# Layer 3 of a four-layer graph network: the 0/1 mask of edges and slots is copied to PSUM and read there by VectorE's products

## The chip, the core and the metric

The kernel runs on one core of one Trainium2 chip. A core has five engines that work in parallel, each through its own queue of instructions: TensorE (PE, matrix products), VectorE (DVE), ScalarE (ACT), GpSimd (POOL, which here issues all gathers and scatters by index) and SyncE (SP, which issues the plain transfers). The metric is the device time of one execution in microseconds (us); lower is better. Operands lie in HBM, in SBUF (the working memory of 128 partitions) or in PSUM (the memory that TensorE writes its results to[...]).

## The reference, cut to what matters

A graph of 12,500 nodes and 212,500 edges goes through four layers, each followed by a layer norm of the sum with its input. Layers 0 to 2 are a weighted sum over edges, an edge network with batch norms, and two graph convolutions. Layer 3, which the change touches, makes six steps. In each, every edge has a 32x32 matrix of its own, made from its attributes by a small network, and multiplies its source node's state; the messages are summed per destination and update the node by a GRU:

```python
eh = relu(e_feat @ en1_w.T + en1_b)                    # (edges, 128)
w_e = (eh @ en2_w.T + en2_b).reshape(-1, D, D)         # D = 32
for _ in range(STEPS):                                 # 6
    msg = einsum('ei,eio->eo', out[src], w_e)
    agg = segment_sum(msg, dst, num_segments=n_nodes) + conv_bias
    h = gru_cell(relu(agg), h, ...)
    out = h
```

## The kernel before, in words

The edges are first sorted by destination, and padded to 212,992: 128 partitions times J = 1664 columns. A column holds 128 neighbouring edges of the sorted order, one per partition, and these have at most 13 destinations (W); otherwise another branch runs, which this input doesn't take. Within a column, each edge has a slot of 0 to 12 for its destination. A chunk is CB = 32 columns, and there are NCH = 52 chunks.

`slot_sum` (line 838) walks over the chunks, for layer 2's convolutions and for each step of layer 3. For each chunk VectorE makes the `mask` (line 848): for 128 edges, 32 columns and 13 slots it is 1 where the edge has that slot. It has three buffers in SBUF. Then a function `fill` puts the sums per slot into `acc` in PSUM, and `then` (line 857) carries them across columns: `on` (L858), a copy out of `acc` by ScalarE (L869), a running sum (`s`, L871), a reordering (L881), eight small matmuls (`back`, L888), and a store.

For layer 3 `fill` is the one in `conditioned` (line 1047). It never makes the edges' matrices. With `eh` (128 values per edge, stored once in HBM) and the gathered states `g`, each half of a chunk (16 columns) goes so:

- POOL gathers the rows of the table `t3` into `g`, one indirect DMA for each column (helper `gather`, L258), so 16 per half and 32 per chunk. A row has the state (32 values) and the state times the bias matrix (32 more). `g` has three buffers of half a chunk.
- SyncE loads `eh` for the half (L1064), also with three buffers.
- For each pair of columns, VectorE multiplies states and mask into `prod` (L1068): for each of 2 columns, 32 features times 13 slots, 832 values per partition. TensorE multiplies `eh` by `prod` into `m` in PSUM (L1076, one matmul for each column; the profile has each fp32 matmul as two records), and ScalarE moves `m` to `outer` in SBUF (L1083). `prod` and `m` have two buffers each.
- The second matmuls of a half (`second`: L1094, 32 of them with `outer` and the weights `en2_i`, and L1104, 16 with `g` and `mask`) are put off until the following half's pairs have been issued, and after the second half of a chunk they are followed by `then`.

Between the loops of two steps lie 98 gathers of the slot ends into `agg` (L258 again), the GRU, and the writing of a new `t3`.

The order within each engine's queue is not written out by hand: the framework's scheduler makes it from the program's order, the dependencies and the free buffers, and puts in the waits. So three masks are made at the beginning of a step, and from then on, in the middle of a chunk, the mask of the chunk after next, beside the `on` and `s` of earlier chunks. [...]

The `mask` is read at two places: by the products (L1068) and by the matmuls of L1104.

Of the kernel before, what the change touches and what calls it, by code (L numbers as in the profile page):

```python
# [32 lines left out]
F32 = mybir.dt.float32  # L33
# [3 lines left out]
AF = mybir.ActivationFunctionType  # L37
# [4 lines left out]
P = 128  # L42
# [4 lines left out]
CB = 32  # L47
# [7 lines left out]
F = 32  # L55
# [3 lines left out]
W = 13  # L59
CW = CB * W  # L60
HB = CB // 2
# [10 lines left out]
def tile_gnn(ctx: ExitStack, tc: tile.TileContext, a: dict, out: bass.AP):  # L72
    nc = tc.nc
# [5 lines left out]
    def sb(pool, shape, dt, name, **kw):  # L79
        return pool.tile(shape, dt, name=name, tag=name, **kw)  # L80
# [488 lines left out]
    with ExitStack() as by_source:  # L569
# [98 lines left out]
        with ExitStack() as l1:  # L668
            n1 = l1.enter_context(tc.tile_pool(name="n1b", bufs=1))
            work = l1.enter_context(tc.tile_pool(name="l1", bufs=3))  # L670
# [167 lines left out]
    def slot_sum(name, rows, table, fill, agg):  # L838


        with tc.tile_pool(name=f"sl_{name}", bufs=2) as work, tc.tile_pool(
            name=f"slp_{name}", bufs=2, space=PSUM
        ) as psum:
            prev = [None]

            def one(c):
                mask = sb(work, [P, CB, W], F32, "mask", bufs=3)
                nc.vector.tensor_tensor(  # L848
                    mask,
                    slot[:, c * CB : (c + 1) * CB].unsqueeze(2).to_broadcast([P, CB, W]),  # L850
                    iota_w.unsqueeze(1).to_broadcast([P, CB, W]),
                    op=ALU.is_equal,
                )
                acc = sb(psum, [rows, CB, W], F32, "acc")

                def then():
                    on = sb(work, [rows, W, CB + 1], F32, "on")
                    nc.vector.tensor_tensor(  # L858
                        on,
                        going[0:rows, c, :].unsqueeze(1).to_broadcast([rows, W, CB + 1]),  # L860
                        iota_w[0:rows, :].unsqueeze(2).to_broadcast([rows, W, CB + 1]),
                        op=ALU.is_equal,
                    )
                    part_ = sb(work, [rows, W, CB + 1], F32, "part")
                    if prev[0] is None:
                        nc.vector.memset(part_[:, :, 0:1], 0.0)
                    else:
                        nc.vector.tensor_copy(part_[:, :, 0], prev[0][:, :, CB])
                    nc.scalar.activation(part_[:, :, 1:], acc.rearrange("p t w -> p w t"), AF.Copy)  # L869
                    s = sb(work, [rows, W, CB + 1], F32, "s")  # L870
                    nc.vector.tensor_tensor_scan(  # L871
                        s.rearrange("p w t -> p (w t)"),
                        on.rearrange("p w t -> p (w t)"),
                        part_.rearrange("p w t -> p (w t)"),
                        initial=0.0,
                        op0=ALU.mult,
                        op1=ALU.add,
                    )
                    prev[0] = s
                    by8 = sb(work, [rows, CB // 8, W, 8], F32, "by8")  # L880
                    nc.scalar.activation(  # L881
                        by8.rearrange("p b w t -> p w b t"),
                        s[:, :, 1:].rearrange("p w (b t) -> p w b t", t=8),
                        AF.Copy,
                    )
                    back = sb(psum, [R8, CB // 8, F], F32, "back", bufs=1)
                    for b in range(CB // 8):
                        nc.tensor.matmul(  # L888
                            back[:, b, :],
                            by8[:, b].rearrange("p w t -> p (w t)"),  # L890
                            stack[0:rows, :],
                            start=True,
                            stop=True,
                        )
                    o = sb(work, [R8, CB // 8, F], F32, "o")
                    nc.scalar.activation(o, back, AF.Copy)
                    n = CB // 8
                    nc.sync.dma_start(
                        table[0:SLOTS, :].rearrange("(r b) f -> r b f", r=R8)[:, c * n : (c + 1) * n, :], o
                    )  # L900

                fill(work, psum, c, mask, acc, then)

            for c in range(NCH):
                one(c)
            fill(None, None, None, None, None, None)
        for c in range(NH):
            gather(agg[:, c, :], table, slot_end[:, c : c + 1])

# [122 lines left out]
                new_table()  # L1032

    def convolved(name, table, nr, agg):
        def fill(work, psum, c, mask, acc, then):
            if work is None:
                return
            g = sb(work, [P, CB, F], F32, "g", bufs=3)
            for j in range(CB):
                gather(g[:, j, :], tables[table], idx_d[:, c * CB + j : c * CB + j + 1])  # L1040
            for j in range(CB):
                nc.tensor.matmul(acc[:, j, :], g[:, j, :], mask[:, j, :], start=True, stop=True)  # L1042
            then()

        slot_sum(f"l2{name}", F, sums[nr], fill, agg)

    def conditioned(agg):
        waiting = []

        def fill(work, psum, c, mask, acc, then):  # L1050
            def flush():
                while waiting:
                    waiting.pop(0)()

            if work is None:
                flush()
                return
            for b in range(2):
                t0 = c * CB + b * HB
                g = sb(work, [P, HB, 2 * F], F32, "g", bufs=3)  # L1060
                for j in range(HB):
                    gather(g[:, j, :], tables["t3"], idx_d[:, t0 + j : t0 + j + 1])
                eh = sb(work, [P, HB, EH], F32, "eh", bufs=3)
                nc.sync.dma_start(eh, edge_h[:, t0 : t0 + HB, :])  # L1064
                outer = sb(work, [EH, F, HB, W], F32, "outer")
                for j in range(0, HB, 2):
                    prod = sb(work, [P, 2, F, W], F32, "prod")
                    nc.vector.tensor_tensor(  # L1068
                        prod,
                        g[:, j : j + 2, 0:F].unsqueeze(3).to_broadcast([P, 2, F, W]),  # L1070
                        mask[:, b * HB + j : b * HB + j + 2, :].unsqueeze(2).to_broadcast([P, 2, F, W]),
                        op=ALU.mult,
                    )
                    m = sb(psum, [EH, 2, 512], F32, "m")
                    for i in range(2):
                        nc.tensor.matmul(  # L1076
                            m[:, i, 0 : F * W],
                            eh[:, j + i, :],
                            prod[:, i].rearrange("p f w -> p (f w)"),
                            start=True,  # L1080
                            stop=True,
                        )
                    nc.scalar.activation(  # L1083
                        outer[:, :, j : j + 2, :].rearrange("k f t w -> k t f w"),
                        m[:, :, 0 : F * W].rearrange("k t (f w) -> k t f w", w=W),
                        AF.Copy,
                    )
                flush()

                def second(b=b, g=g, outer=outer):  # L1090
                    af = acc.rearrange("p t w -> p (t w)")
                    for i in range(F):
                        q = i % 4
                        nc.tensor.matmul(  # L1094
                            af[q * F : (q + 1) * F, b * HW : (b + 1) * HW],
                            en2_i[:, i, :],
                            outer[:, i].rearrange("k t w -> k (t w)"),
                            start=i < 4,
                            stop=False,
                            skip_group_check=True,  # L1100
                        )
                    for j in range(HB):
                        q = j % 4
                        nc.tensor.matmul(  # L1104
                            acc[q * F : (q + 1) * F, b * HB + j, :],
                            g[:, j, F:],
                            mask[:, b * HB + j, :],
                            start=False,
                            stop=True,
                            skip_group_check=True,  # L1110
                        )
                    if b == 1:
                        then()

                waiting.append(second)

        slot_sum("l3", P, sums[0], fill, agg)


# [142 lines left out]
```

## Time and profile before

| what | value |
|---|---|
| timed runs, median of 3 | 39500.57 us (39438.2 to 39509.71) |
| profiled execution, own time | 34886.39 us |
| profiled execution, span from the first to the last instruction | 34884.6 us |
| TensorE clock granted, mean | 0.744 of full speed |
| busy: POOL / PE / DVE / ACT | 23436.5 / 17930.9 / 10465.9 / 7279.3 us |
| the six loops of gathers of layer 3 | 19424.1 to 34580.2 us, each 2296 to 2318 us long |

Times in the profile come from one execution under the hardware profiler. It took less time than the timed runs did, by 4614 us; the profile doesn't say where. A group in the profile is all instructions of one line, engine and operation on the same tiles: its count, its busy time, the mean length of one, and the idle time of its engine just before them with what ended that. In the timeline a line is one instruction: its start in us from the beginning of the span, its length, and in brackets how long its engine had stood idle and what released it. "Issue" is time in which an engine waited for nothing that the profile shows. L258 means line 258 of the kernel, and as this is a helper's line, groups are told apart by their tiles.

### The profile page before, as it was taken

How to read it: one execution, taken by the hardware profiler on the slowest of the kernel's cores; microseconds unless marked ns; L12 is line 12 of the kernel's file. 1: busy time of each engine (PE TensorE's matmuls, PEld its weight loads, DVE VectorE, ACT ScalarE, POOL GpSimd, SP SyncE). 2: the span in 40 equal slices, each digit the busy share in tenths (PEclk: the TensorE clock that was granted, in tenths of full speed). 3: DMA queues.
4: the chain of work that ended last, by engine and by line, in shares of the span. 5: the costliest groups of instructions: out<-in, count | busy, mean ns of one | idle time of the engine just before them, and what ended most of it. 6: DMA issues, size and time to landing. Idle time of an engine off the chain costs nothing. (4 is left out here: it accounts for less than half of the span.)

```text
span 34884.6 us, 317851 instructions
## 1 busy us (share of the span) xinstructions
PE 17930.9 (51%) x121935; PEld 10224.7 (29%) x121935; DVE 10465.9 (30%) x12313; ACT 7279.3 (21%) x11783; POOL 23436.5 (67%) x22620
## 2 busy tenths in 40 slices
PE   3666664000000039922222577676776776776776
PEld 3555554000000012211111333343343333343333
DVE  9544443111000030000000343343443443443443
ACT  0222221000000041100000233233332332332332
POOL 0777666776777730077777677677677676776776
PEclk6877777555555565555555899999999998998998
DMA  0000111110000032200000222222222221221221
GB/s 11 2 2 5 22 22 28 25 24 23 20 20 20 20 103 83 82 15 15 15 15 15 65 72 66 65 73 63 68 73 59 71 74 54 75 74 54 76 73 54
DMA packets 1176160, 1562.93 MB, mean 45 GB/s; under 512 B 663528, under 2 KB 885484, under 8 KB 1085804
## 3 DMA queue, kind: packets, MB, share of 16 engines
q1 hardware_dynamic: 451052, 1029.85, 8.5%
q0 software_dynamic: 723584, 512.50, 7.2%
q8 instruction: 989, 16.20, 0.2%
q14 instruction: 535, 4.38, 0.0%
HBM read 1257.04 MB, written 283.77 MB: 44 GB/s over the span
## 5 line engine op out<-in xcount | busy, mean ns | idle before, releaser
L258 POOL DMA_INDIRECT g<-t,idx_d x9984 | 10805.4, 1082 | 3733.3 <-issue 2891.6
L1076 PE MATMUL m<-prod,eh 128*128 128x416 f32 x19968 | 8324.6, 553 | 3097.6 <-DVE prod L1068 3050.6
L1068 DVE TENSOR_TENSOR prod<-g,mask 128x832 f32<-128x832 f32 x4992 | 5151.2, 1035 | 8054.3 <-DMA g<-t,idx_d 5914.6
L1083 ACT ACTIVATE outer<-m 128x832 f32<-128x832 f32 x4992 | 4488.4, 899 | 6891.4 <-PE m L1076 6887.3
L1076 PEld LDWEIGHTS m<-prod,eh 128*128 128x128 f32 x19968 | 3631.7, 200 | 7182.5 <-issue 4414.1
L258 POOL DMA_INDIRECT g<-t2a,idx_d x1664 | 1592.3, 957 | 2168.1 <-DMA t2a<-own 1661.5
L382 POOL DMA_INDIRECT rec_s<-rows_s,pos x1664 | 1906.7, 1146 | 1457.5 <-DVE pos L432 950.7
L1042 PE MATMUL acc<-mask,g 128*32 128x13 f32 x6656 | 933.9, 218 | 3151.3 <-DMA g<-t2a,idx_d 1579.1
L382 POOL DMA_INDIRECT rec_d<-record,row_d x1664 | 1743.7, 1048 | 872.5 <-issue 490.6
L686 PE MATMUL t<-ident,gp 128*128 128x128 f32 x416 | 110.5, 441 | 4074.1 <-DVE gp L680 4074.1
L258 POOL DMA_INDIRECT g<-t,rs x1664 | 1709.3, 1027 | 508.8 <-issue 492.0
L258 POOL DMA_INDIRECT g<-t2b,idx_d x1664 | 1593.1, 957 | 554.9 <-issue 492.0
L258 POOL DMA_INDIRECT gp<-t1p,rs x1664 | 1571.4, 944 | 577.6 <-issue 492.0
L258 POOL DMA_INDIRECT gq<-t1q,rs x1664 | 1588.3, 955 | 506.9 <-issue 506.9
L1094 PE MATMUL acc<-outer,en_i 128*32 128x208 f32 x39936 | 1893.7, 342 | 0.0
L410 PE MATMUL same<-xt 128*128 128x128 f32 x6656 | 1482.5, 338 | 497.1 <-ACT xt L407 497.1
L421 PE MATMUL place<-cur,xt 128*128 128x98 f32 x6652 | 1640.5, 340 | 183.8 <-ACT cur L427 171.6
L427 ACT ACTIVATE cur<-next 128x98 f32<-128x98 f32 x3326 | 837.6, 252 | 4139.2 <-PE next L422 2493.6
L1042 PEld LDWEIGHTS acc<-mask,g 128*32 128x32 f32 x6656 | 601.9, 140 | 3479.7 <-DMA g<-t2b,idx_d 1660.5
L1094 PEld LDWEIGHTS acc<-outer,en_i 128*32 128x32 f32 x39936 | 1240.9, 110 | 777.2 <-issue 374.9
L848 DVE TENSOR_TENSOR mask<-slot,iota_w 128x416 f32<-128x416 bf16 x416 | 244.3, 588 | 3741.1 <-PE acc L1042 3729.4
L421 PEld LDWEIGHTS place<-cur,xt 128*128 128x128 f32 x6652 | 1213.0, 227 | 498.5 <-ACT cur L427 467.5
(316 smaller groups left out, 18565.6 us busy)
## 6 DMA issues: line engine op xcount, KB each, us to landing
eh<-edge_h SPq DMA_DIRECT2D x624, 1024.0 KB
g<-t,idx_d POOLq DMA_INDIRECT x9984, 2.5
edge_h<-eh SPq DMA_DIRECT2D x52, 2048.0 KB
scan<-o SPq DMA_DIRECT2D x104, 512.0 KB
ht<-h_t SPq DMA_DIRECT2D x104, 512.0 KB
rd<-rec_d SPq DMA_DIRECT2D x52, 544.0 KB
record<-in_edge_attr SPq DMA_DIRECT2D x52, 512.0 KB
rec_s<-rows_s,pos POOLq DMA_INDIRECT x1664, 2.1
```

Source lines behind the costliest of these rows:

```text
L258: nc.gpsimd.indirect_dma_start(out=to, out_offset=None, in_=table, in_offset=bass.IndirectOffsetOnAxis(ap=idx, axis=0))
L382: i = nc.gpsimd.indirect_dma_start(out=to, out_offset=bass.IndirectOffsetOnAxis(ap=idx, axis=0), in_=data, in_offset=None)
L410: nc.tensor.matmul(same[:, j, :], xt[:, j, :], xt[:, j, :], start=True, stop=True)
L421: nc.tensor.matmul(place[:, j, :], xt[:, j, :], cur, start=False, stop=True)
L427: nc.scalar.activation(cur, nxt, AF.Copy)
L686: nc.tensor.transpose(t[:, g, :], gp[:, jj : jj + 4, :].rearrange("p j f -> p (j f)"), ident)
L848: nc.vector.tensor_tensor(mask, slot[:, c * CB : (c + 1) * CB].unsqueeze(2).to_broadcast([P, CB, W]), iota_w.unsqueeze(1).to_broadcast([P, ...
L1042: nc.tensor.matmul(acc[:, j, :], g[:, j, :], mask[:, j, :], start=True, stop=True)
L1068: nc.vector.tensor_tensor(prod, g[:, j : j + 2, 0:F].unsqueeze(3).to_broadcast([P, 2, F, W]), mask[:, b * HB + j : b * HB + j + 2, :].unsq ...
L1076: nc.tensor.matmul(m[:, i, 0 : F * W], eh[:, j + i, :], prod[:, i].rearrange("p f w -> p (f w)"), start=True, stop=True,)
L1083: nc.scalar.activation(outer[:, :, j : j + 2, :].rearrange("k f t w -> k t f w"), m[:, :, 0 : F * W].rearrange("k t (f w) -> k t f w", w=W ...
L1094: nc.tensor.matmul(af[q * F : (q + 1) * F, b * HW : (b + 1) * HW], en2_i[:, i, :], outer[:, i].rearrange("k t w -> k (t w)"), start=i < 4, ...
```

## The change

In `slot_sum`, where it is called with 128 rows (layer 3 alone; layer 2 calls it with 32), ScalarE copies the chunk's `mask` to a new PSUM tile `near`, with one buffer. `near` is handed to `fill`, and layer 3's products read it in place of `mask`. Layer 2's `fill` takes the argument and doesn't use it. The matmuls of L1104 still read `mask` in SBUF.

```diff
@@ slot_sum, in one(c), behind the making of mask
                 acc = sb(psum, [rows, CB, W], F32, "acc")
+                near = None
+                if rows == P:
+
+                    near = sb(psum, [P, CB, W], F32, "near", bufs=1)
+                    nc.scalar.activation(near, mask, AF.Copy)
...
-                fill(work, psum, c, mask, acc, then)
+                fill(work, psum, c, mask, near, acc, then)
@@ convolved and conditioned
-        def fill(work, psum, c, mask, acc, then):
+        def fill(work, psum, c, mask, near, acc, then):
@@ conditioned, the product
                     nc.vector.tensor_tensor(
                         prod,
                         g[:, j : j + 2, 0:F].unsqueeze(3).to_broadcast([P, 2, F, W]),
-                        mask[:, b * HB + j : b * HB + j + 2, :].unsqueeze(2).to_broadcast([P, 2, F, W]),
+                        near[:, b * HB + j : b * HB + j + 2, :].unsqueeze(2).to_broadcast([P, 2, F, W]),
                         op=ALU.mult,
                     )
```

More of the change, by code (lines that the diff above doesn't have):

```diff
@@ L900, in then @@
                     )
-                fill(work, psum, c, mask, acc, then)
+                fill(work, psum, c, mask, near, acc, then)
             for c in range(NCH):
                 one(c)
-            fill(None, None, None, None, None, None)
+            fill(None, None, None, None, None, None, None)
         for c in range(NH):
@@ L1048, in conditioned, with fill @@
         waiting = []
-        def fill(work, psum, c, mask, acc, then):
+        def fill(work, psum, c, mask, near, acc, then):
             def flush():
```

## The prediction

> **What bounds the kernel now.** I read the costliest groups first, then POOL's own waits, the table by stretches, and last the timeline. Costliest groups (busy us, mean ns of one, idle before):
>
> ```profile
> L258 POOL DMA_INDIRECT g<-t,idx_d x9984 | 10805.4, 1082 | 3733.3 <-issue 2891.6
> L1076 PE MATMUL m<-prod,eh 128*128 128x416 f32 x19968 | 8324.6, 553 | 3097.6 <-DVE prod L1068 3050.6
> L1068 DVE TENSOR_TENSOR prod<-g,mask 128x832 f32<-128x832 f32 x4992 | 5151.2, 1035 | 8054.3 <-DMA g<-t,idx_d 5914.6
> L258 POOL DMA_INDIRECT g<-t2b,idx_d x1664 | 1593.1, 957 | 554.9 <-issue 492.0
> ```
>
> Layer 3's 9984 gathers take 1082 ns each, layer 2's 957; the 784 gathers of slot ends, beside which no product runs, take 944 (740.1 us). The products wait chiefly for gathers, TensorE for products. POOL's own waits (total us, times, longest):
>
> ```profile
> POOL g L258 <- issue: 4367.6, 14335, 0.3
> POOL g L258 <- DVE mask L848: 693.0, 6, 120.3
> ...
> POOL g L258 <- DMA g<-t,idx_d: 93.3, 306, 0.3
> ...
> POOL g L258 <- PE m L1076: 26.2, 86, 0.3
> ```
>
> Within a step POOL waits for nobody: only the 0.30 us of issue before each gather, whatever the name behind it; the six waits of 120 us lie between steps. The gather loop of one step, by engine (PE, PEld, DVE, ACT, POOL busy; clock; DMA):
>
> ```profile
> 22006.00:24302.00 2296.00, 1754.51 (x13520) 903.30 (x13520) 962.19 (x1035) 811.26 (x984) 1789.25 (x1664) 0.96 0.24 73
> ```
>
> 1789 busy + 1664 x 0.30 = 2289 of 2296 us: POOL sets this stage. TensorE has 24% left. One of the 52 chunks takes 44.2 us here; the loops of all six steps sum to 13846 us, a mean of 44.4. Now the timeline inside layer 3 (start, duration; TensorE left out):
>
> ```profile
> 26512.99 1.03 DVE L1068 TENSOR_TENSOR prod<-g,mask 128x832 f32<-128x832 f32 x1 [0.99 <-DMA g<-t,idx_d]
> 26513.13 1.70 POOL L258 DMA_INDIRECT g<-t,idx_d  x1 [0.30 <-issue]
> ...
> 26515.14 0.94 POOL L258 DMA_INDIRECT g<-t,idx_d  x1 [0.30 <-issue]
> 26516.39 0.94 POOL L258 DMA_INDIRECT g<-t,idx_d  x1 [0.30 <-issue]
> 26516.44 1.02 DVE L1068 TENSOR_TENSOR prod<-g,mask 128x832 f32<-128x832 f32 x1 [2.42 <-DMA g<-t,idx_d]
> ...
> 26518.82 1.03 DVE L1068 TENSOR_TENSOR prod<-g,mask 128x832 f32<-128x832 f32 x1 [1.35 <-DMA g<-t,idx_d]
> 26518.89 1.78 POOL L258 DMA_INDIRECT g<-t,idx_d  x1 [0.30 <-issue]
> ```
>
> A gather that begins inside a product ends about 0.82 us after the product (26514.02 to 26514.83; 26519.85 to 26520.67), as if it had stood still until then; one that begins 50 ns ahead of the product takes 0.94. Over all of layer 3, 2454 gathers begin 60 ns or more inside a product, at a mean of 1384 ns; those with no vector work beside them take 944. The sort stage has the counter-test, POOL's scatters beside other products:
>
> ```profile
> 953.58 3.41 DVE L311 TENSOR_TENSOR oh_hi<-iotab,khi_s 128x3136 bf16<-128x3136 bf16 x1
> 953.73 4.11 POOL L382 DMA_INDIRECT rec_s<-rows_s,pos  x1 [0.30 <-issue]
> ...
> 959.05 0.57 DVE L429 TENSOR_TENSOR own<-place,oh_hi 128x392 f32<-128x392 f32 x1 [1.58 <-PE next L422]
> 959.41 0.96 POOL L382 DMA_INDIRECT rec_s<-rows_s,pos  x1 [0.30 <-issue]
> ```
>
> `iotab` and `khi_s` are both in SBUF: the scatter stands still. `place` is in PSUM, only `oh_hi` in SBUF: the scatter, begun 0.36 us inside, takes its ordinary 0.96. Of L429 and L412 (also one PSUM input) I counted 628 POOL operations begun inside; all took 952 to 975 ns but one (1130).
>
> [...]
>
> **The change part by part.**
> 1. Copy. 52 x 6 = 312 ScalarE copies 128x416, priced by the nearest rows, L869 0.52 us and L881 0.55: 312 x 0.52 = 162 us. ScalarE is busy 811 of 2296 us in a step; this adds 27. Behind it on ScalarE stand evictions of `m`, for which TensorE waits. On the path: 0, hidden by POOL's 40 us per chunk.
> 2. New wait. `near` has one buffer, so the copy waits for the chunk's last product, and the next chunk's first product for the copy. At 26519.85 a chunk's last product ends, and the last eviction at 26522.56. Copy behind it: 23.08; product: 24.1. TensorE, at the older half's second matmuls, takes up the next chunk's product only at 26524.84. So 0.7 us is over and the wait costs 0; without that cover it is 0.9 + 0.52 + 1.03 = 2.5 us a chunk, against TensorE's slack (below).
> 3. Products. The same 4992 instructions. [...] I take 0. VectorE is busy 18.5 of 44.4 us a chunk, so neither end is on the path.
> 4. POOL. Above 944 ns stands 138 ns x 9984 = 1378 us. What stays: masks L848, `on` L858 and scans L871 still read two SBUF inputs. Layer 2 runs the same three per chunk without a product and stands 13 ns over: 13 x 9984 = 130 us. Bounds: 65 us (the gathers now begun inside those three, times their excess) and 195 (half as much again, as in layer 3 the three stand in one block). I take 130: a gain of 125 ns x 9984 = 1248 us.
> 5. What is late next. The chunk becomes 32 x (0.957 + 0.30) = 40.2 us. TensorE is busy 33.8 us a chunk. POOL has three buffers of half a chunk and never waited for one, so TensorE's lateness within a half doesn't reach it. Landing, table, GRU and slot ends are unchanged.
>
> Sum: 34886.4 - 1248 = 33638 us for the profiled execution. The timed runs' median is 39500.6, 4614 more, and their excess is in no trace. I carry the difference over as constant: 39500.6 - 1248 = **38250 us**.
>
> **Rivals.**
> A. The timed runs lose more to the block than the profile does. Every product can hold a gather by at most 1.79 - 0.944 = 0.85 us; the profile shows 0.28 per product. For: in undisturbed stretches products begin within 50 ns of a gather's start, on the edge between free and blocked, so that a landing slightly earlier blocks every time; and 4614 us need an owner. Against: no view shows it. With half of the products blocking in full, 2496 x 0.85 - 130 = 1990 us are gained: 37510.
> B. TensorE takes over part way. Its 33.8 us a chunk grow by the bubbles after each half's second matmuls (1.2 to 1.8 us of waiting for `prod`), and the copy adds its 2.5. If a chunk settles at 42.4 us, 2.0 x 312 = 620 us are gained: 38880. Against: most of TensorE's waits are for late gathers, which come earlier.
> C. No release: the PSUM operand with its repeated rows still excludes POOL: 39500. Against: the 628 cases.
> D. Slower: the single `near` buffer turns each chunk's end into a full drain. It decides once the TensorE chain passes 44.4 us, a further 44.4 - 33.8 = 10.6 us a chunk; at 12 us, 1.4 x 312 = 440 us are lost: 39940. Against: four times the 2.5 us that I can find; it would take a copy queued behind evictions of the next chunk.
>
> **How the numbers follow.** This measurement can tell about 0.2% (79 us) from no change. Likeliest case, gain 0.9 to 1.6 ms, 37900 to 38600: 0.60. A, gain over 1.6 ms: 0.14. B, gain 0.08 to 0.9 ms: 0.15. C, within 0.2%: 0.03. D, slower: 0.08. So faster 0.89, same 0.03, slower 0.08. The range 37000 to 39000 holds the likeliest, most of A (up to 2.5 ms) and two thirds of B (from 0.5 ms): 0.60 + 0.11 + 0.10. What remains outside is D, C and the tails.
>
> **What would show it.** Right: the gathers' mean falls from 1082 to about 957 ns; a gather begun inside a product takes 944; POOL's waits within a step remain 0.30 us of issue; a step's loop shortens from 2308 to about 2095 us; the span is near 33640. Step 1 or 2 is wrong if products wait long for `near`, or TensorE for products at a chunk's first pair. Step 3 is wrong if the product takes over 1.10 us. Step 5 is wrong if POOL shows waits for buffers that TensorE releases, or TensorE's busy share nears 100%. The prediction falls if the mean stays at 1082, if a chunk stays above 42 us, or if the timed runs move by an amount far from the profile's own.

## The result, and the profile after

The changed kernel takes 40423.43 us (median of 4 runs, 40383.57 to 40424.65), the kernel before 39505.14 us beside it. The ratio is 1.0234, 95% interval 1.0216 to 1.0252: slower, where 38250 us were forecast, outside the range and on its other side.

First the costliest groups of the changed kernel (busy us, mean ns of one, idle before). L1073 is now the product, L1081 the matmul behind it, L1099 and L1109 are the second matmuls, L859 the copy.

```profile
L258 POOL DMA_INDIRECT g<-t,idx_d x9984 | 9489.8, 951 | 7318.4 <-PE acc L1109 3736.2
L1081 PE MATMUL m<-prod,eh 128*128 128x416 f32 x19968 | 7734.7, 544 | 308.1 <-DVE prod L1073 161.9
L1073 DVE TENSOR_TENSOR prod<-g,near 128x832 f32<-128x832 f32 x4992 | 5092.9, 1020 | 6653.1 <-PE m L1081 4939.3
L1099 PE MATMUL acc<-outer,en_i 128*32 128x208 f32 x39936 | 4729.7, 427 | 3163.9 <-issue 3120.8
...
L859 ACT ACTIVATE near<-mask 128x416 f32<-128x416 f32 x312 | 162.7, 521 | 48.5 <-issue 39.8 <-DVE prod L1073 7.9
```

The gathers did what the prediction said: 1082 ns became 951. The product takes 1020 ns from PSUM, the copy 0.52 us. But the products now wait for TensorE (4939.3 us), not for gathers (433.8; TensorE itself has only 308 us of idle time before L1081), and POOL stands idle for 3736 us behind L1109. Most telling is L1099, a group that the prediction did not look at. This is it in the profile from which the prediction was made:

```profile
L1094 PE MATMUL acc<-outer,en_i 128*32 128x208 f32 x39936 | 1893.7, 342 | 0.0
```

The same 39936 records now have 3164 us of idle time before them, almost all of it "issue", that is, with nothing in the profile to wait for. The waits of the changed kernel (total us, times, longest):

```profile
PEld acc L1099 <- issue: 5347.5, 5897, 3.4
DVE prod L1073 <- PE m L1081: 4939.3, 2370, 14.9
POOL g L258 <- issue: 4315.8, 14081, 0.9
POOL g L258 <- PE acc L1109: 3736.2, 606, 21.1
...
DVE prod L1073 <- ACT near L859: 22.5, 38, 0.7
```

606 times POOL waits for the end of a half chunk's second matmuls, because L1109 reads the `g` buffer that POOL wants next. The products waited for `near` for 22.5 us in all. The gather loop of one step (PE, PEld, DVE, ACT, POOL busy; clock; DMA):

```profile
28536.00:31220.00 2684.00, 2102.82 (x13426) 1069.35 (x13427) 956.30 (x1029) 829.04 (x1027) 1580.97 (x1664) 0.83 0.23 63
```

It takes 2684 us where 2095 were forecast: 1581 + 1664 x 0.30 = 2080 us are POOL's, the other 604 are its waits. The six loops sum to 16084 us, 51.6 us a chunk. The timeline shows one such block of second matmuls (start, duration; other instructions between left out):

```profile
28707.13 1.66 PE L1099 MATMUL acc<-outer,en_i 128*32 128x208 f32 x32
28707.57 0.94 POOL L258 DMA_INDIRECT g<-t,idx_d  x1 [0.30 <-issue]
...
28709.68 0.34 PE L1099 MATMUL acc<-outer,en_i 128*32 128x208 f32 x1 [0.89 <-issue]
28710.07 0.94 POOL L258 DMA_INDIRECT g<-t,idx_d  x1 [0.30 <-issue]
...
28711.83 0.35 PE L1099 MATMUL acc<-outer,en_i 128*32 128x208 f32 x1 [0.36 <-issue]
28712.51 0.42 PE L1099 MATMUL acc<-outer,en_i 128*32 128x208 f32 x1 [0.33 <-issue]
...
28713.81 0.94 POOL L258 DMA_INDIRECT g<-t,idx_d  x1 [0.30 <-issue]
28713.91 0.50 PE L1099 MATMUL acc<-outer,en_i 128*32 128x208 f32 x1 [0.98 <-issue]
...
28717.41 2.34 PE L1099 MATMUL acc<-outer,en_i 128*32 128x208 f32 x24 [0.89 <-issue]
...
28720.71 0.94 POOL L258 DMA_INDIRECT g<-t,idx_d  x1 [5.95 <-PE acc L1109]
```

TensorE begins the block with 32 records in 1.66 us. Then it falls to one record in 0.7 us, or in twice that, while gathers run. The last gather ends at 28714.75, TensorE runs without a break again from 28717.41, and POOL, whose buffer the block frees, has waited 5.95 us. I call this the crawl. It is tied to the gathers: over the 606 halves in which POOL waits so, the last stall of TensorE ends 2.7 us after POOL's last gather (median; 2.6 to 2.7 in the middle half of them). In the first profile of the kernel before there is no crawl (0.0 us of idle time before L1094).

### The profile page after: what moved, and what is told of

Read it like the earlier page. It is cut to its first block, busy times and chain, and to the rows that moved or that the text cites. A ratio compares the mean times of both kernels' runs of the same rounds, so it can differ in the third digit from the quotient of the medians.

```text
span 40420.4 us, 318169 instructions
## 1 busy us (share of the span) xinstructions
PE 20144.0 (50%) x121935; PEld 11386.9 (28%) x121935; DVE 10464.7 (26%) x12313; ACT 7437.5 (18%) x12095; POOL 22267.2 (55%) x22620
## 5 line engine op out<-in xcount | busy, mean ns | idle before, releaser
L258 POOL DMA_INDIRECT g<-t,idx_d x9984 | 9489.8, 951 | 7318.4 <-PE acc L1109 3736.2
L1081 PE MATMUL m<-prod,eh 128*128 128x416 f32 x19968 | 7734.7, 544 | 308.1 <-DVE prod L1073 161.9
L1073 DVE TENSOR_TENSOR prod<-g,near 128x832 f32<-128x832 f32 x4992 | 5092.9, 1020 | 6653.1 <-PE m L1081 4939.3
L1099 PE MATMUL acc<-outer,en_i 128*32 128x208 f32 x39936 | 4729.7, 427 | 3163.9 <-issue 3120.8
L1081 PEld LDWEIGHTS m<-prod,eh 128*128 128x128 f32 x19968 | 3651.6, 201 | 3798.7 <-issue 2913.6
L1099 PEld LDWEIGHTS acc<-outer,en_i 128*32 128x32 f32 x39936 | 2047.8, 129 | 5726.8 <-issue 5347.5
L382 POOL DMA_INDIRECT rec_s<-rows_s,pos x1664 | 1704.3, 1024 | 2693.2 <-DVE pos L432 2201.5
L410 PE MATMUL same<-xt 128*128 128x128 f32 x6656 | 1682.8, 374 | 1297.9 <-issue 676.2
L848 DVE TENSOR_TENSOR mask<-slot,iota_w 128x416 f32<-128x416 bf16 x416 | 245.3, 591 | 7997.3 <-PE acc L1109 3582.9
L258 POOL DMA_INDIRECT gp<-t1p,rs x1664 | 1785.3, 1073 | 664.8 <-issue 557.6
L1047 PE MATMUL acc<-mask,g 128*32 128x13 f32 x6656 | 552.6, 204 | 2330.6 <-issue 2125.0
L410 PEld LDWEIGHTS same<-xt 128*128 128x128 f32 x6656 | 1245.1, 248 | 1455.8 <-ACT xt L407 740.0
```

What stands on the lines that cost most here:

```text
L258: nc.gpsimd.indirect_dma_start(out=to, out_offset=None, in_=table, in_offset=bass.IndirectOffsetOnAxis(ap=idx, axis=0))
L382: i = nc.gpsimd.indirect_dma_start(out=to, out_offset=bass.IndirectOffsetOnAxis(ap=idx, axis=0), in_=data, in_offset=None)
L410: nc.tensor.matmul(same[:, j, :], xt[:, j, :], xt[:, j, :], start=True, stop=True)
L848: nc.vector.tensor_tensor(mask, slot[:, c * CB : (c + 1) * CB].unsqueeze(2).to_broadcast([P, CB, W]), iota_w.unsqueeze(1).to_broadcast([P, ...
L1073: nc.vector.tensor_tensor(prod, g[:, j : j + 2, 0:F].unsqueeze(3).to_broadcast([P, 2, F, W]), near[:, b * HB + j : b * HB + j + 2, :].unsq ...
L1081: nc.tensor.matmul(m[:, i, 0 : F * W], eh[:, j + i, :], prod[:, i].rearrange("p f w -> p (f w)"), start=True, stop=True,)
```

## The experiments

e1 and e2 ran on one chip (number 7), e3 to e6 on chip 3, e7 to e11 on chip 8, e12 to e14 on chip 5, e15 and e16 on chip 13; each with runs of the kernel before beside it. On which chip the first profile of the kernel before and that of the changed kernel were taken is not on record.

**The kernel before again, and the copy alone.** e1 changes nothing. e2 makes the copy and leaves the products at the mask:

```diff
-    near[:, b * HB + j : b * HB + j + 2, :].unsqueeze(2).to_broadcast([P, 2, F, W]),
+    mask[:, b * HB + j : b * HB + j + 2, :].unsqueeze(2).to_broadcast([P, 2, F, W]),
```

> The kernel before, unchanged, profiled once more. The changed kernel's second matmuls of a half (32 in a block) take 12.2 us a block in its profile, against 2.7 in the first profile of before, and layer 2, whose code is the same, is slower as well. Theory 1 (the first profile of before was an execution in which TensorE's blocks of small matmuls ran undisturbed, and the timed runs of before are not like it): the span is near 39500 us, the blocks take about 12 us here too, a step's gather loop about 2545 us, and POOL waits for TensorE within a step. Theory 2 (the change itself makes the blocks slow): the blocks take 2.7 us, the span is near 34900.

> ScalarE copies the mask to near, but the products read the mask in SBUF as before: nothing reads near. Theory A (the copy itself, on ScalarE ahead of the evictions of m, costs the time): about 40400 us, 2% over before. Theory B (what costs is that the products read PSUM: either they wait for the one buffer of near, or POOL, no longer held, runs into TensorE's time): within 0.3% of before, 39500 us, with gathers still at a mean of 1000 ns or more.

Measured: e1 39515.55 us (one run), e2 39503.95 us, a ratio of 1.0001 (0.9992 to 1.001) to the kernel before beside it. So the copy costs nothing, and the whole loss comes with the products' new operand. The groups and waits of e1, the kernel before:

```profile
L258 POOL DMA_INDIRECT g<-t,idx_d x9984 | 10453.3, 1047 | 5444.9 <-issue 2767.2 <-PE acc L1104 1865.2 <-DVE mask L848 721.6
L1076 PE MATMUL m<-prod,eh 128*128 128x416 f32 x19968 | 8376.0, 580 | 213.1 <-DVE prod L1068 129.8 <-issue 53.2 <-DMA eh<-edge_h 21.6
L1094 PE MATMUL acc<-outer,en_i 128*32 128x208 f32 x39936 | 3273.2, 356 | 1215.4 <-issue 1153.5
```
```profile
DVE prod L1068 <- PE m L1076: 5868.8, 4635, 16.8
...
POOL g L258 <- PE acc L1104: 1865.2, 606, 10.0
```

This is the kernel before as it is timed, and it differs from the profile that the prediction read: the crawl is there too, POOL waits 606 times for TensorE, and a chunk takes 48.6 us, not 44.4. It also shows where nearly all of the 4614 us lie that the prediction could not place. Layer 3 begins at 22633 us instead of 19424 (3209 us, in code that the change does not touch), and its six loops take 15177 us instead of 13846 (1331 us).

Set against e1, the loops of the changed kernel take 907 us more (16084 - 15177), which is all of the difference of the two spans (40420 - 39514). Per half chunk, of which there are 624: the 16 gathers take 16 x (1047 - 951) = 1.5 us less; POOL's waits for the second matmuls go from 1865 to 3736 us in all, 3.0 us more. For TensorE, whose matmuls of L1081 have only 308 us of idle time before them, a half is a block of second matmuls and then the 16 columns' matmuls. The block goes from 10.7 to 13.0 us, the matmuls from 13.4 to 12.4 (8376 and 7734.7 us over 624).

**Half of the gathers.** Every second gather of layer 3 is left out, and products and L1109 use the neighbour's rows (these two edits are left out here).

```diff
-                for j in range(HB):
+                for j in range(0, HB, 2):
                     gather(g[:, j, :], tables["t3"], idx_d[:, t0 + j : t0 + j + 1])
...
```

> The changed kernel with every second gather of layer 3 left out (the odd columns of a pair take the even column's states, so its result is another; every other instruction is there). In the changed kernel each block of small second matmuls of a half starts at full speed, then gets on by about one instruction in 0.7 us, and comes back to full speed some 2.6 us after POOL's last gather before a wait. Theory 1 (the crawl lasts as long as gathers are under way): POOL's 8 gathers of a half take 10 us, are over before the block begins, and the block takes about 3 us instead of 12.6; a chunk takes 34 to 38 us instead of 51.6 and the span is near 35500 us. Theory 2 (the crawl comes from TensorE's own stream of instructions, or from the load of eh): the block still takes over 8 us, and the chunk stays above 45 us.

> The changed kernel with every second gather of layer 3 left out, as before on another chip (there: 30575 us, blocks of second matmuls at full speed). On a chip where before takes 39500 us or more: theory 1 (the blocks crawl as long as gathers are under way) expects blocks of about 3 us and chunks of 34 to 38 us; theory 2 (they crawl for a reason of TensorE's own stream, or beside the load of eh) expects blocks of over 8 us and chunks above 45 us. On a chip where before takes 34550: as before.

Measured, one run each: 30575.44 us on chip 3, where the kernel before takes 34554.47; 33926.12 us on chip 8, where it takes 39699.13. The group of second matmuls in e9:

```profile
L1099 PE MATMUL acc<-outer,en_i 128*32 128x208 f32 x39936 | 1885.5, 340 | 0.0
```

On the chip with the crawl, the crawl is gone: no idle time before L1099, a block of 3.3 us as expected, and 30.7 us a chunk against 30.5 on chip 3, less than the 34 to 38 expected. With 8 gathers a half, POOL has finished 2.2 us before the block begins and waits for its end. So these matmuls don't crawl by themselves on that chip: with no gather beside them they take 340 ns each, where they take 430 in e8, the changed kernel there, and have 3331 us of idle time before them. The two runs still differ by 3351 us, of which 0.25 x 312 = 78 us are in these loops and nearly all the rest ahead of layer 3.

**A pause per gather.** A small POOL memset is issued for each gather, to slow POOL down without VectorE.

```diff
                 for j in range(HB):
                     gather(g[:, j, :], tables["t3"], idx_d[:, t0 + j : t0 + j + 1])
+                    if j % 1 == 0:
+                        idle = sb(work, [P, 16], F32, "idle")
+                        nc.gpsimd.memset(idle, 0.0)
```

> The changed kernel with a POOL memset of 128x16 after each gather of layer 3, which gives the gathers about the pace they have before the change (1.35 us from one to the next instead of 1.25). The products still read PSUM and hold nobody. Theory P (the cost of the change is the faster pace of the gathers, against TensorE's blocks): the time comes back to about before, 39300 to 39700 us. Theory Q (the cost is in reading near itself, its one buffer or its PSUM bank): it stays at 40400 us or above.

> The changed kernel with a POOL memset of 128x16 after each gather of layer 3, as before on another chip (there: 0.997 of before). On a chip where before takes 39500 us or more: theory P (what costs is the faster pace of the gathers) expects 39300 to 39700 us, theory Q (what costs is reading near, its one buffer or its bank) 40400 us or more. On a chip where before takes 34550: a ratio of 0.997 again.

Measured: 34447.03 us, a ratio of 0.9967 (0.9955 to 0.998) on chip 3; 41111.07 us, 1.0357 (1.034 to 1.0374), on chip 8. Both miss their purpose: the scheduler put nearly all of the memsets together in lumps of 65 to 154, and the gathers between them still came every 1.25 us. They only added their own 817 us of busy POOL time. The time of e11 lies where theory Q had it, but as the pace was not changed, it decides nothing between P and Q.

**The second matmuls spread out.** Six of the second matmuls are issued behind each pair of columns of the next half, instead of all 48 behind the last pair (of the edit, the lines that set the order).

```diff
+                older = waiting.pop(0) if waiting else []
                 for j in range(0, HB, 2):
                     ...
-                flush()
+                    for piece in older[3 * j : 3 * j + 6]:
+                        piece()
+                for piece in older[3 * HB :]:
+                    piece()
```

> The changed kernel with the second matmuls of a half no longer in one block behind the next half's pairs, but six at a time behind each pair; nothing else differs. Theory 1a (small matmuls crawl only in a long run of them while gathers are under way): TensorE keeps up, POOL's 40.2 us set the chunk, and 11 us x 312 are gained: about 37000 us. Theory 1b (every small matmul crawls beside gathers, run or not): the 48 of a half all crawl, and the time is 42000 us or more.

> The same spreading in the kernel before (products read the mask in SBUF and hold POOL). Theory 1a: TensorE keeps up, and POOL with its held gathers sets the chunk, 44 us or more: 37900 to 38500 us, so that the change would then gain about 1200 us. Theory 1b: 41000 us or more.

> The changed kernel with the second matmuls six at a time behind each pair, as before on another chip (there: 0.972 of before). On a chip where before takes 39500 us or more: theory 1a (only a long run of small matmuls crawls beside gathers) expects about 36500 to 37500 us; theory 1b (each small matmul crawls beside gathers) expects 42000 us or more. On a chip where before takes 34550: a ratio of 0.972 again.

Measured: on chip 3 the changed kernel so spread takes 33593.1 us, a ratio of 0.9718 (0.9702 to 0.9734), and the kernel before so spread 34469.21, 0.9974 (0.9966 to 0.9983). On chip 8 the former takes 42347.56 us, 1.0662 (1.0645 to 1.068), with 57.4 us a chunk. Chip 3 has no crawl, so it couldn't tell 1a from 1b; there the place of the small matmuls matters little (0.3% for the kernel before). On chip 8 the time lies in the range of 1b, and the small matmuls of L1102, six at a time, have 951.6 us of idle time before them (4.5 on chip 3): the crawl is there without a long run of them. That the block fares better because part of it falls into POOL's idle time is my explanation, and no run tests it.

**The changed kernel again.** Without an edit, on three more occasions.

> The changed kernel, unchanged, once more, beside the kernel before on the same chip. The runs so far fall into two kinds by the chip they ran on: one on which the kernel before takes about 39500 us and TensorE's blocks of small matmuls crawl, and one on which it takes about 34550 us and they don't. Theory 1 (the change gains where TensorE's blocks run freely, and loses where they crawl beside the gathers): on a chip of the second kind, where before takes about 34550, the changed kernel takes about 33350 us, a ratio of 0.962 to 0.972; on one of the first kind 40420, a ratio of 1.023. Theory 2 (the change loses by itself, whatever the chip): a ratio of 1.01 or more on either.

> The changed kernel once more. If this chip is one where the kernel before takes about 34550 us: 33350 us, a ratio of 0.962 to 0.972, with POOL waiting for nobody within a step. If it is one where before takes 39500 to 39750: a ratio near 1.023 again.

> The changed kernel unchanged, beside the two before on the same chip. 40400-40700 us, a ratio of 1.022 to 1.026, where the kernel before takes 39500-39750; where that takes about 34550, this takes 33200-33600, a ratio of 0.960 to 0.973, as my prediction's POOL gain of 1248 us has it.

Measured: 40691.05 us (1.0238, interval 1.0221 to 1.0255) and 40660.83 us (1.0244, 1.0227 to 1.0261) on chip 8, 33636.34 us (0.9724, 0.9708 to 0.974) on chip 5. The groups and waits of e14:

```profile
L258 POOL DMA_INDIRECT g<-t,idx_d x9984 | 9560.0, 958 | 3734.5 <-issue 2848.8
...
L1073 DVE TENSOR_TENSOR prod<-g,near 128x832 f32<-128x832 f32 x4992 | 5079.9, 1020 | 6895.3 <-DMA g<-t,idx_d 5081.4
...
L1099 PE MATMUL acc<-outer,en_i 128*32 128x208 f32 x39936 | 1886.5, 341 | 0.0
```
```profile
POOL g L258 <- issue: 4327.5, 14193, 0.3
```

So one and the same change is 2.8% faster on chip 5 and 2.4% slower on chip 8. This is theory 1 of e7; in e14 the ratio is within the range expected, the time 36 us above it. On chip 5 the gathers take the 957 ns of the prediction (958), POOL waits for nobody within a step, and the span is 33635.5 us, where 33638 were worked out for the profiled execution (in part by luck: see step 4 below). Every chip but number 8 was used on one occasion only, and the two on chip 8 were 18 minutes apart. So whether the crawl belongs to the chip, or to something else that differed between these occasions, is not shown; "a chip with the crawl" means no more than this.

**POOL held again, or the same work from PSUM.** What remained was why the change loses where there is a crawl: because POOL is no longer held by the products, so that gathers come faster and more of them run unheld, or because the products read PSUM. To the changed kernel a product of 416 elements is added behind each product, its output unused. In e12 and e15 both of its inputs are in SBUF, in e13 and e16 the second is `near`. The diff has the two edits one below the other, with comments added and one line shortened.

```diff
+                    tmp = sb(work, [P, F, W], F32, "tmp")
+                    nc.vector.tensor_tensor(tmp, prod[:, 0], prod[:, 1], op=ALU.mult)       # e12, e15
+                    nc.vector.tensor_tensor(tmp, prod[:, 0], near[:, b * HB + j, :]...,     # e13, e16
+                                            op=ALU.mult)
                     m = sb(psum, [EH, 2, 512], F32, "m")
```

> The changed kernel, with one VectorE product of 416 elements put behind each of layer 3's products: both its inputs are in SBUF (the two columns of prod), and its output is not used. It holds POOL's gathers again, while the products themselves still read PSUM. Theory 1 (where the blocks of small matmuls crawl beside gathers, the change loses because POOL is no longer held, and so more unheld gathers run ahead of and beside a block): the gathers' mean rises from 951 to 1000-1100 ns, the instructions that a block gets done before its first stall rise from 65 towards 105, POOL's waits for a block's end over 1 us shrink from 3831 us towards 1960, and the total falls from about 40660 to 39600-40300 us, in spite of the added work. Rival (it loses because the products read PSUM): the blocks stay at 60-70 instructions before the stall, and the total is 40660 us or more. On a chip without the crawl: slower than the changed kernel by what POOL is held, 33900-34600 us.

> The counter-test: the same added VectorE product of 416 elements in the same place, but with its second input in PSUM (near), so that it doesn't hold POOL and doubles half of the reading of PSUM. Theory 1 (pace): gathers stay at 945-960 ns, a block has 60-70 instructions before its stall, and the total is within 0.5% of the changed kernel's on the same chip (about 40500-40900 us). Rival (reading of PSUM): the loss grows by about half, so 40950-41300 us, with fewer instructions before the stall. On a chip without the crawl: 33200-33700 us, as the changed kernel.

> The kernel of e12 again, for a chip with the crawl (the kernel before at 39500-39750 us), where the changed kernel stands at a ratio of 1.023-1.024. Theory 1 (pace): ratio 0.997-1.015, over 75 instructions of a block before its first stall. Rival (reading of PSUM): ratio 1.023 or more, 60-70 instructions. Where the kernel before takes about 34550: 0.986 again, which tells nothing new.

> The kernel of e13 again, for a chip with the crawl. Theory 1 (pace): ratio 1.018-1.029, 60-70 instructions before the stall. Rival (reading of PSUM): 1.031-1.040. Where the kernel before takes about 34550: 0.973 again.

| chip | kernel before | both in SBUF (holds POOL) | second in PSUM |
|---|---|---|---|
| 5, no crawl | 34586.37 us | 34110.71 us, 0.9862 (0.9845 to 0.9878) | 33680.79 us, 0.9734 (0.9718 to 0.9751) |
| 13, crawl | 39477.68 us | 40196.06 us, 1.0187 (1.017 to 1.0204) | 40366.16 us, 1.0227 (1.021 to 1.0244) |

The gathers on chip 5, e12 and then e13:

```profile
L258 POOL DMA_INDIRECT g<-t,idx_d x9984 | 10049.5, 1007 | 3735.3 <-issue 2829.1
```
```profile
L258 POOL DMA_INDIRECT g<-t,idx_d x9984 | 9603.1, 962 | 3737.3 <-issue 2844.0
```

The gathers and POOL's waits on chip 13, first e15:

```profile
L258 POOL DMA_INDIRECT g<-t,idx_d x9984 | 9841.4, 986 | 6703.1 <-PE acc L1111 3127.8 <-issue 2762.7 <-DVE mask L848 718.1
...
L1080 DVE TENSOR_TENSOR tmp<-prod 128x416 f32<-128x416 f32 x4992 | 2844.8, 591 | 84.8
```

and then e16:

```profile
L258 POOL DMA_INDIRECT g<-t,idx_d x9984 | 9490.1, 951 | 7271.9 <-PE acc L1111 3694.5 <-issue 2799.1 <-DVE mask L848 719.5
...
L1080 DVE TENSOR_TENSOR tmp<-prod,near 128x416 f32<-128x416 f32 x4992 | 2928.7, 587 | 171.0
```

The two added products take the same time. The one from PSUM leaves the gathers at 951 ns and the total where the changed kernel has it (1.0227 against 1.0234 to 1.0244): more reading of PSUM costs nothing that shows, and the rival, which expected 1.031 to 1.040, falls. The one from SBUF lengthens the gathers to 986 ns, and yet the kernel is 170 us quicker than its twin: POOL's waits for L1111 are 3127.8 us against 3694.5, 0.91 us a half less, for 0.56 us (16 x 35 ns) of longer gathers. On chip 5 the same pair has the opposite sign, and the hold costs 430 us, near to (1007 - 962) ns x 9984 = 449 us. Holding POOL a little is a loss without the crawl and a gain with it.

The size was missed: 0.997 to 1.015 was expected of e15, and it gave 1.0187. The added product holds POOL for 35 ns a gather, 36% of the 96 ns that the old products did, and it gives back 216 of the 866 us by which the loops of e16 (16042 us) exceed those of e1, 25% (e1 ran on chip 7, where the kernel before is within 0.1% of chip 13). That the rest would come back with a full hold is plausible, and not shown. The expected number of records before a block's first stall can't be read here, since the added work moved the start of each block ahead of the last pair's matmuls. What can be read is how many of a block's 192 records (matmuls and weight loads) have begun when the half's last gather ends, on the mean of the halves in which POOL waits: about 137 in e1, 79 after the change, 77 in e16, 93 in e15; the rest of the block then takes about another 2.2, 5.3, 5.2 and 4.3 us.

## Why the prediction was wrong, step by step

1. Copy: right. 312 copies of 0.521 us, and e2's ratio of 1.0001.
2. Wait for the one buffer of `near`: right, 22.5 us in the whole kernel.
3. Products from PSUM: right that nothing is added: 1020 ns, against 1029 in e1 and the 1035 from which the prediction started. What the trace before had to go by were other products: L848, 588 ns for 416 elements with its inputs in SBUF, and L429, 563 ns for 392 with one of them in PSUM.
4. POOL's gain: right in mechanism. The 3902 gathers that begin 60 ns or more inside a product now take 944 ns (1384 before), and the mean is 951 to 958 against 957 forecast. So what the 628 operations beside L429 and L412 had shown, that a product with one operand in PSUM doesn't hold POOL, the trace after shows for these products as well. The size was too large even where there is no crawl. On chip 5, beside the kernel before (34586 us), the gain was 950 us, three quarters of the 1248; with the second matmuls spread out on chip 3 it was 876 (e6 to e5). That the span of e14 comes within 3 us of the 33638 worked out is in part luck, since the profile it started from took 300 us more than the kernel before takes on chips 3 and 5; why it did is not known.
5. What is late next: wrong in the timed runs. "POOL has three buffers of half a chunk and never waited for one, so TensorE's lateness within a half doesn't reach it" was read from a profile in which a block of 48 second matmuls takes 3.3 us from its first start to its last end (as in e14, which has no crawl either). It takes 10.7 us in e1 and 13.0 after. "TensorE is busy 33.8 us a chunk" counted busy time, and the crawl is in the main idle time between instructions. The prediction's own sign that step 5 is wrong, waits of POOL for buffers that TensorE releases, came 606 times.

The sum then failed at "I carry the difference over as constant". The 4614 us were no constant lying beside the loops. 1331 of them were in layer 3's loops, and they were the sign that there the owner of the chunk was another engine: 48.6 us a chunk against the 44.4 of POOL. So the 1.5 us a half that POOL gained went into its own wait for TensorE. That alone, as I estimate, would have made no difference. The loss came because the gain made that wait longer: fewer of the block's instructions get through before the last gather ends (79 of 192 instead of 137), and the remainder is done after it, at POOL's cost. That the missing hold is what does this is shown by e15 against e16 for a quarter of the loss, and argued for the rest: the copy (e2), the wait for `near` (22.5 us) and more reading of PSUM (e16) are no causes.

The rivals. A sought the 4614 us in the products' hold; they were not there. B named the right engine, but as a limit to the gain, not as a loss. C is excluded by step 4. D had the sign and its deciding point, a TensorE chain over 44.4 us a chunk, which e1 had already passed at 48.6; its mechanism, the drain of `near`, was not what passed it. No rival was that the other 4614 us could mean another bound, although the text said that their excess is in no trace.

What stays open: why small matmuls crawl beside gathers on chips 7, 8 and 13 and not on 3 and 5. The profile calls it issue, and no view names what TensorE's queue waits for; none of the stalled instructions of the blocks in the changed kernel's profile has a semaphore to wait for (of its 39936 weight loads of L1099, 6 have one). A slow load of instructions would be one candidate, but the 989 packets of queue q8, which the profile calls instruction, took 1.06 us each in the first profile of the kernel before, without the crawl, and 1.12 in the changed kernel's. The granted clock doesn't explain it: one record in 0.7 us is 13 times slower than 32 in 1.66 us, and from the first to the last gather of layer 3 the clock was 0.84 in e1 and 0.85 in e16, whose loops are 866 us longer (0.93 in e14).

One thing separates the traces of the two kinds without exception: those with the crawl hold 76,000 to 123,000 events of DMAs landing, the others 306,000 to 385,000, for programs that issue nearly the same DMAs (e3 and e9, the same program, 306,078 and 75,759). So what the crawl traces put down to a DMA, or to none, is less sure than in the others, and whether the loss of these events and the crawl have one cause, the recording itself among them, no run tests.

How the faster gathers bring the crawl on earlier is shown only in its effect (e15 against e16). No version here beats the kernel before on both kinds of chip.

## What to carry to other kernels

When the profiled execution and the timed runs differ by far more than the change can bring (here by 4614 us, against 1248), the profile may show another bound than the one that is timed: profile the kernel again until the two agree before working out anything. Idle time put down to issue, in front of a long row of small instructions (3120.8 us before L1099), belongs in the sum of an engine's time as much as its busy time does. Ask which engine owns the period before counting what another is freed of: POOL, freed of the products' hold, gained where it owned the period (950 us on chip 5); where TensorE did, the block of second matmuls beside the faster gathers went from 10.7 to 13.0 us, and the loops lost 907 us.

## What was not expected of the hardware

The same kernel on chips 3 and 5 takes 34554 and 34586 us, on chips 7, 8 and 13 39477 to 39750, 14 to 15% more. 3209 us of that were there before layer 3 began (e1 against the first profile). In layer 3 it shows as TensorE falling to steps of about 0.7 us while indirect gathers run, with one record of L1099 a step in the block shown above; on chip 8 without gathers beside them (e9) the same instructions take 340 ns, on chip 5 with all gathers (e14) 341, and have no idle time before them in either.
